# A four-layer image network in one kernel: the second layer's SyncE queue put in written order, two loads moved, a zeroing split

## The chip, the cores and the metric

The kernel runs on one core of a Trainium2 chip. The metric is the device time of one execution in microseconds; lower is better. Single executions are compared by their median.

## What is computed

The input is eight images of 56 x 56 points and 192 channels in fp32. Four layers follow one another, each of the form `x = x + layer(groupnorm(x))`: a gated convolution along rows and columns, an attention over 3 x 3 neighbourhoods, a windowed attention, and a recurrence along rows, columns and diagonals. The change lies in the second layer, whose reference is:

```python
v = x @ Wv
vp = jnp.pad(v, ((0, 0), (1, 1), (1, 1), (0, 0)))
patches = stack of the 9 shifted views of vp at stride 2      # (B, 28*28, 9, 6 heads, 32)
pooled = 2x2 mean of x
a = softmax((pooled @ Wa + ba).reshape(B, 28*28, 6, 9, 9) * scale, axis=-1)
out = einsum('bnhpq,bnqhd->bnphd', a, patches)
y = the 9 parts of out added back at their shifted places     # fold
return y @ Wp + bp
```

## The kernel before, in words

The engines are PE (matrix products), DVE and POOL (element-wise work), ACT (functions and copies) and SP (SyncE), which here only starts DMAs. The second layer, `layer1`, works on 28 units: 4 pairs of images by 7 strips of 8 image rows. Work on a unit is spread over several rounds of one loop over `n` (PE's order within a round is `attend(n)`, the logits of n+2, `values` of n+1, `fold(n)`):

- `load(n)` (L989) brings a unit's input into one of six buffers `x`, with six DMAs. `load(n + 4)` stands first in round n, so it takes the buffer of unit n-2.
- `normalize(n + 3)` applies the group norm on ACT (L1033, three instructions) and pools 2 x 2 points on POOL. `patches(n + 2)` copies nine shifted views into `xc` on DVE, ACT and POOL.
- `attend(n)` multiplies the unit's values `v` by a block-diagonal matrix of attention weights, `bds[n % 2]` (PE, L1155); ACT copies the result out of PSUM into `ys` (L1164).
- `attention(n + 2)` makes the weights: `logits` on PE, DVE and POOL (L1074 to L1085), then `weights` (exponential on ACT L1088, sums on DVE L1089, L1090, product on POOL L1094 into `aq`). SP stores `aq` to a DRAM tile `ad` (L1099), the weights' store.
- `spread(n + 2)` (L1112) reads `ad` back with 14 small DMAs that place the weights on the block diagonals of `bds[n % 2]`. The rest of `bds` is zero and is set to zero once, before the loop.
- `values(n + 1)` (L1126) multiplies the patches by `Wv` in four steps; each needs a bank of PSUM that ACT has to copy out first (L1130).
- `fold(n)` multiplies `ys` by `Wp`, DVE adds it to `x` (L1220), and `finish(n - 1)` stores unit n-1 with six DMAs (L1179) and takes its statistics (L1183). The last strip of a pair finishes its own unit too: twelve stores in that round, none in the next.

Before the loop the first two units are prepared ("the entry"): loads of units 0 to 3, weights of units 0 and 1, and their spreads, which SP and POOL share seven DMAs each. Fetches of norms (L995, L996) and of the next layer's weights (L1279 to L1283) are SP's as well.

The order of the instructions is set in two ways. PE, DVE, ACT and POOL run in the order in which the code is written: `tc.manual_schedule` is entered for them at the top of the layer. SP isn't among them: its DMAs are put in order by a planner, which simulates the kernel with its own costs and issues what it finds ready. An engine executes its queue strictly in order, and an instruction that waits holds up all behind it. SP's first DMA of a spread waits until `ad` has landed in DRAM, and until PE has read the old `bds`; the first DMA of a load waits until the stores of the unit whose buffer it takes have landed. In the third layer's first stage SP is in written order already (L1606).

Of the kernel before, what the change touches and what calls it, by code (L numbers as in the profile page):

```python
# [926 lines left out]
def layer1(cx, xin, xout, w, consts):  # L927
# [9 lines left out]
    tc, nc = cx.tc, cx.nc  # L937
# [5 lines left out]
    NG = 2 * NR  # L943
# [12 lines left out]
    with ExitStack() as es:  # L956
# [13 lines left out]
        E = mybir.EngineType  # L970
# [3 lines left out]
        def parts(x, p, t):  # L974

            cols = slice(t * SW, (t + 1) * SW)
            for i in range(2):
                d = 2 * p + i
                yield x[0:CP, i], d, (slice(None), 0, cols)
                yield x[CP:CA, i], d, (slice(0, CA - CP), 1, cols)  # L980
                yield x[sides[i], 2], d, (slice(CA - CP, None), 1, cols)
# [3 lines left out]
        def load(n, queue=nc.sync):  # L985
            if n < len(units):
                xs[n] = cx.tile(xp, [128, 3, SW], "x")
                for dst, d, at in parts(xs[n], *units[n]):
                    queue.dma_start(dst, xin[d][at])  # L989

        def fetch_norms(p, queue):
            norms[p] = cx.tile(cp, [128, 3, 2], f"norm{p}")
            for i in range(2):
                src = cx.norms[2 * p + i]
                queue.dma_start(norms[p][:, i, :], src[0:CA])  # L995
                queue.dma_start(norms[p][sides[i], 2, :], src[CA:])  # L996
# [24 lines left out]
        bds = [cx.tile(cp, [NP, 2 * NG, NCOL, HEADS, 3], f"bd{i}") for i in range(2)]  # L1021

        def normalize(n):

            p, t = units[n]
            x, xn = xs[n], xns[n % 2]
            if t == 0:
                nc.gpsimd.memset(xn[:, 0, :, 1, :], 0.0)
            else:
                nc.gpsimd.tensor_copy(xn[:, 0, :, 1, :], xns[(n - 1) % 2][:, NR, :, 1, :])  # L1030
            for j in range(3):
                s, o = norms[p][:, j, 0:1], norms[p][:, j, 1:2]
                nc.scalar.activation(  # L1033
                    xn[:, 1:, j, :, 1:], x[:, j].rearrange("p (y i x) -> p y i x", i=2, x=H),
                    AF.Identity, bias=o, scale=s,
                )
            rows = cx.tile(sp, [128, NR, 3, H], "rows")
            nc.gpsimd.tensor_tensor(rows, xn[:, 1:, :, 0, 1:], xn[:, 1:, :, 1, 1:], ALU.add)
            pool4 = cx.tile(wk, [128, 3, NR, N], "pool")
            nc.gpsimd.tensor_tensor(  # L1040
                pool4.rearrange("p j y x -> p y j x"), rows[:, :, :, 0:H:2], rows[:, :, :, 1:H:2], ALU.add
            )
            return pool4.rearrange("p j y x -> p j (y x)")

        def patches(n):

            xn = xns[n % 2]
            xc = cx.tile(wk, [128, 3 * NR, 2, KK, NX], "xc")
            for q in range(KK):
                j, i = divmod(q, 3)  # L1050
                src = xn[:, (i + 1) // 2 : (i + 1) // 2 + NR, :, (i + 1) % 2, j : j + 2 * N - 1 : 2]
                src = src.rearrange("p y j (u x) -> p (y j) u x", u=2)
                dst = xc[:, :, :, q, :]
                if q in (3, 7):
                    nc.gpsimd.tensor_copy(dst, src)
                elif q in (1, 5):
                    nc.scalar.copy(dst, src)
                else:
                    nc.vector.tensor_copy(dst, src)
            return xc  # L1060
# [45 lines left out]
        def spread(n, ad, queues=(nc.sync, nc.sync)):  # L1106

            av = ad.rearrange("i (g x) q f -> x q (i g) f", x=NX)
            bd = bds[n % 2].rearrange("p g c h i -> p g (c h i)")
            for x in range(NX):  # L1110
                at = 2 * x * 3 * HEADS
                queues[x % 2].dma_start(bd[x : x + (KK - 1) * NX + 1 : NX, :, at : at + HK], av[x])  # L1112
# [29 lines left out]
        def attend(n, v):  # L1142


            bd, t = bds[n % 2], units[n][1]
            py = cx.tile(psy, [128, 3, 512], "y")
            for g in range(NG):
                r, half = divmod(g, 2)
                i0 = int(t == 0 and r == 0)
                c0 = int(half == 0)  # L1150
                dims = (NCOL - c0, 3 - i0)
                to = (half * 2 * NX + c0 - 1) * NY + 2 * r + i0
                for k, block in enumerate(blocks):
                    for u, (i, h) in enumerate(block):
                        nc.tensor.matmul(  # L1155
                            sub(py[u * HD : (u + 1) * HD, k, to:], (NY, dims[0]), (1, dims[1])),
                            v[:, i, g, h * HD : (h + 1) * HD],
                            bd[:, i * NG + g, c0:, h, i0:],
                            start=(g == 0), stop=True, skip_group_check=True,
                        )  # L1160
            ys = cx.tile(sp, [128, 3, NY, H], "ys")
            lo = int(t == 0)
            src = py[:, :, 0 : NY * H].rearrange("p j (x y) -> p j y x", y=NY)
            nc.scalar.copy(ys[:, :, lo:, :], src[:, :, lo:, :])  # L1164
            if t:
                nc.gpsimd.tensor_tensor(ys[:, :, 0, :], ys[:, :, 0, :], carry.pop(0), ALU.add)
            if t < NT - 1:
                carry[0] = cx.tile(sp, [128, 3, H], "carry", bufs=2)
                nc.gpsimd.tensor_copy(carry[0], ys[:, :, NY - 1, :])
            return ys  # L1170
# [58 lines left out]
        for i, xn in enumerate(xns):  # L1229
            nc.gpsimd.memset(xn[:, :, :, :, 0], 0.0)  # L1230
        nc.gpsimd.memset(bds[0][:, 0:NG], 0.0)
        pools[0] = normalize(0)
        xcs[0] = patches(0)
        warm = cx.tile(sp, [1, 1], "warm")
# [14 lines left out]
            f()  # L1249
        second = attention(pools.pop(1), ads)  # L1250
        second[0]()
        spread(0, ads.pop(0), (nc.sync, nc.gpsimd))
        vs[1] = cx.tile(wk, [NP, 2, NG, C], "v")
        todo = values(xcs.pop(1), vs[1])
# [3 lines left out]
        pools[2] = normalize(2)  # L1258
        for f in todo:
            f()  # L1260
        nc.vector.memset(bds[1], 0.0)
        spread(1, ads.pop(), (nc.sync, nc.gpsimd))
        gn = cx.gn = GroupNormPairs(cx, cx.keep, w["gmat"])
        gn.place = psb, "b"
# [6 lines left out]
        for n in range(len(units)):  # L1271
            if n == 2:
                for f in cx.late:
                    f(lambda: cx.tile(psb, [128, 512], "b"))
                fetch_norms(NPAIR - 1, nc.sync)
            load(n + 4)
            if n == 20:
                for t, name in zip(cx.held, ("W_vb0", "W_vb1")):
                    nc.sync.dma_start(t, consts[f"l2_{name}"])  # L1279
                nc.sync.dma_start(cx.held[2], consts["l2_b_vb"].partition_broadcast(128))  # L1280
                for i in range(2):
                    nc.sync.dma_start(gn.first[:, i, :], cx.norms[i][0:CA])
                    nc.sync.dma_start(gn.first[sides[i], 2, :], cx.norms[i][CA:])  # L1283
            if n + 3 < len(units):
                pools[n + 3] = normalize(n + 3)
            if n + 2 < len(units):
                xcs[n + 2] = patches(n + 2)
            ys = attend(n, vs.pop(n))
            if n + 1 < len(units):
                todo = []  # L1290
                if n:
                    vs[n + 1] = cx.tile(wk, [NP, 2, NG, C], "v")
                    todo = values(xcs.pop(n + 1), vs[n + 1])
                if n + 2 < len(units):
                    logits, weights = attention(pools.pop(n + 2), ads)
                    logits()
                    todo.insert(2, weights)
                for f in todo:
                    f()
                if ads:  # L1300
                    spread(n + 2, ads.pop())
            if late and late[0][0] <= n:
                late.pop(0)[1]()
            fold(n, ys)
# [1043 lines left out]
def network(tc, d, out):  # L2348
    cx = Ctx(tc)
    B = d["x"].shape[0]  # L2350
    with ExitStack() as es:
        dp = es.enter_context(tc.tile_pool(name="mid", bufs=1, space=DRAM))
        ims = [[d["x"][b] for b in range(B)]]
        for n in range(3):
            ims.append([cx.tile(dp, [CP, 2, HW], f"x{n}_{b}") for b in range(B)])
        ims.append([out[b] for b in range(B)])
        for n, layer in enumerate((layer0, layer1, layer2, layer3)):
            w = {k[3:]: v for k, v in d.items() if k.startswith(f"l{n}_")}
            layer(cx, ims[n], ims[n + 1], w, d)
# [32 lines left out]
```

## Time and profile before

| what | value |
|---|---|
| median of 3 executions | 3863.78 us (3854.99 to 3865.73) |
| the profiled execution's own time | 3867.67 us |
| its span, first to last instruction | 3865.6 us |
| PE busy over the span | 3706.9 us, 96% |
| DVE, ACT, POOL busy | 2421.6, 1806.9, 1535.1 us |
| the second layer | about 1811 to 2445 us |
| starts of `attend`, n = 0 to 6 | 1847.7, 1864.4, 1893.4, 1915.3, 1935.5, 1955.6, 1976.1 us |
| starts of `attend`, n = 23 to 27 | 2344.7, 2365.8, 2387.9, 2409.9, 2429.4 us |
| share of the 16 DMA engines' time, SP's and ACT's queue q1 | 50.0% |

The difference between the profiled time and its span is what lies around the span, 2 us. In the rows of a timeline the first number is the start in us from the span's start, the second the duration; then come engine, line, operation, names as out<-in, and in brackets how long the engine was idle before and what ended it. `SPq` is SP's queue: a row's duration is the issue of the DMAs, not their transfer. Names leave buffer numbers out, so `x<-x` on L989 is a load and on L1179 a store.

### The profile page before, as it was taken

The numbers are of one execution on the slowest core, as the hardware profiler recorded it, in microseconds if no ns is written. First come the engines' busy times: TensorE is split into PE (matmuls) and PEld (weight loads), VectorE is DVE, ScalarE is ACT, GpSimd is POOL, SyncE is SP. The second block draws the span as 40 slices with busy tenths as digits, with TensorE's granted clock in tenths as the row PEclk, the third lists the DMA queues.
The fourth block names the chain that finished last, engine by engine and source line by source line (L and its number), as shares of the span: only waits on it lengthen the run. The fifth ranks groups of instructions, "written<-read, shape, count | busy, mean of one in ns | idle before, by whom it ended". The sixth has DMA issues, their size and how long they took to land. (4 is left out here: it accounts for less than half of the span.)

```text
span 3865.6 us, 116066 instructions
## 1 busy us (share of the span) xinstructions
PE 3706.9 (96%) x51036; PEld 2639.2 (68%) x51036; DVE 2421.6 (63%) x3267; ACT 1806.9 (47%) x2068; POOL 1535.1 (40%) x1336
## 2 busy tenths in 40 slices
PE   7999999999999999998899999899989999999998
PEld 5777878777777868777667666444435555556997
DVE  5657676665757677556444444665657777775665
ACT  4444455444445445344434433344335555554664
POOL 4232242323233242223433333333335545445776
PEclk9999999999999999999999999999999999999999
DMA  8866363434436263343344343656549767664333
GB/s 161 179 137 159 81 168 89 125 98 106 118 85 172 81 160 90 89 101 102 91 124 103 104 97 98 181 174 204 176 146 208 179 162 174 156 151 120 98 111 103
DMA packets 389502, 508.64 MB, mean 132 GB/s; under 512 B 175848, under 2 KB 325672, under 8 KB 387606
## 3 DMA queue, kind: packets, MB, share of 16 engines
q1 hardware_dynamic: 386502, 496.22, 50.0%
q8 instruction: 401, 6.57, 0.7%
q0 software_dynamic: 1424, 4.14, 0.4%
q10 hardware_dynamic: 1072, 0.87, 0.1%
q14 instruction: 103, 0.84, 0.1%
HBM read 345.38 MB, written 155.65 MB: 130 GB/s over the span
## 5 line engine op out<-in xcount | busy, mean ns | idle before, releaser
L438 POOL TENSOR_TENSOR qv<-s,s 128x392 f32<-128x392 f32 (+3 forms) x320 | 564.8, 1796 | 1171.6 <-ACT s L418 796.7
L410 PE MATMUL c<-x,wqv 64*128 64x392 f32 x2592 | 458.4, 497 | 8.4 <-ACT s L418 4.9
L410 PEld LDWEIGHTS c<-x,wqv 64*128 64x128 f32 x2592 | 244.9, 188 | 161.8 <-ACT s L418 6.2
L418 ACT ACTIVATE s<-c,bqv 128x784 f32<-128x784 f32 (+1 forms) x247 | 224.8, 913 | 223.0 <-PE c L410 214.5
L432 DVE TENSOR_TENSOR qv<-s,s 128x784 f32<-128x784 f32 (+1 forms) x160 | 258.9, 1634 | 98.8 <-ACT s L418 98.8
L552 PE MATMUL c<-x,wp 64*128 64x224 f32 x2688 | 282.9, 356 | 14.0 <-ACT s L559 6.8
L471 ACT COPY or<-c 56x1024 f32<-56x1024 f32 x183 | 183.7, 1008 | 222.1 <-DVE ol L471 220.2
L471 DVE COPY ol<-c 56x1024 f32<-56x1024 f32 x184 | 221.7, 1210 | 84.9 <-PE c L465 84.6
L552 PEld LDWEIGHTS c<-x,wp 64*128 64x128 f32 x2688 | 254.8, 189 | 18.7 <-ACT s L559 9.0
L576 DVE TENSOR_TENSOR s<-s,c 128x896 f32<-128x896 f32 x112 | 121.8, 1088 | 219.1 <-ACT s L559 212.8
L1126 PE MATMUL c<-wv,xc 128*126 128x192 f32 (+1 forms) x1792 | 248.9, 336 | 7.0 <-ACT v L1130 4.4
L1126 PEld LDWEIGHTS c<-wv,xc 128*126 128x126 f32 (+1 forms) x1792 | 218.1, 187 | 46.9 <-issue 36.9
L1686 ACT ACTIVATE vb<-sm 128x1024 f32<-128x1024 f32 (+1 forms) x100 | 103.7, 1040 | 258.1 <-issue 220.0
L559 ACT ACTIVATE s<-c,bp 128x448 f32<-128x448 f32 x224 | 129.9, 631 | 190.5 <-PE c L552 189.6
L1835 POOL TENSOR_TENSOR rs<-rs,sin_win 128x896 f32<-128x896 f32 x56 | 136.2, 2450 | 196.5 <-ACT rs L1824 196.5
L510 PEld LDWEIGHTS c<-or,ol 120*64 120x64 f32 (+1 forms) x6720 | 199.6, 133 | 21.4 <-issue 11.1
L510 PE MATMUL c<-or,ol 120*64 120x56 f32 (+1 forms) x6720 | 207.3, 221 | 6.6 <-ACT or L471 5.6
L2257 POOL TENSOR_TENSOR y<-y,s 128x448 f32<-128x448 f32 x164 | 181.4, 1106 | 79.5 <-ACT s L2227 74.7
L1675 PE MATMUL v<-wvb,wa 128*128 128x512 f32 (+1 forms) x400 | 193.2, 615 | 4.9 <-DVE wa L49 4.9
L2214 PE MATMUL h<-ringh,am 128*64 128x57 f32 (+1 forms) x4304 | 184.8, 232 | 7.8 <-DVE ringh L2220 6.1
L1913 ACT ACTIVATE us<-c,bub 128x896 f32<-128x896 f32 x84 | 84.6, 1008 | 222.1 <-PE c L1895 138.9
L1704 POOL TENSOR_TENSOR l<-vb,ta 128x512 f32<-128x512 f32 (+1 forms) x52 | 74.8, 1438 | 275.4 <-ACT vb L1686 275.4
(293 smaller groups left out, 7948.3 us busy)
## 6 DMA issues: line engine op xcount, KB each, us to landing
or<-tt SPq DMA_DIRECT2D x252, 196.0 KB
ol<-tt SPq DMA_DIRECT2D x252, 196.0 KB
vt<-v SPq DMA_DIRECT2D x56, 672.0 KB
v<-vb SPq DMA_DIRECT2D x96, 384.0 KB
x<-x SPq DMA_DIRECT2D x110, 168.0 KB
wqv<-in_l_w_qv SPq DMA_DIRECT2D x40, 384.0 KB
x<-in_x SPq DMA_DIRECT2D x64, 196.0 KB
x<-x SPq DMA_DIRECT2D x110, 112.0 KB
```

Source lines behind the costliest of these rows:

```text
L410: nc.tensor.matmul(ps[:, h, 0:n], wqv[q][rows, k, i, :], xn[rows, k, g * n : (g + 1) * n], start=(k == 0), stop=(k == 2),)
L418: nc.scalar.activation(t, ps[rows, :, 0:n], AF.Silu, bias=bqv[rows, j : j + 1])
L432: nc.vector.tensor_tensor(sub(qv[rows, 7 * g :, 64 + H - 1 :], (HH * 120, 2), (120, 7), (-1, H)), *(t.rearrange("p u (h w) -> p u h w", w= ...
L438: eng.tensor_tensor(sub(qv[rows, w0:, H - 1 - 7 * g - HH * u :], (120, w1 - w0), (-1, 7)), *(t[:, u].rearrange("p (h w) -> p w h", w=H)[:, ...
L471: copy(dst[:, :, :, i0 : i0 + 8], view[rows])
L510: nc.tensor.matmul(ps[u * 64 : u * 64 + m, k, v * H : (v + 1) * H], left[:, d * H : d * H + m], right[:, d * H : (d + 1) * H], start=True, ...
L552: nc.tensor.matmul(ps[:, h, u * n : (u + 1) * n], wps[j][rows, k, u, :], xn[rows, k, g * n : (g + 1) * n], start=(u == 0 and k == 0), stop ...
L1126: nc.tensor.matmul(out(i, u), group(2 if part else i, u)[rows], wv[part][rows], start=(first and u == 0), stop=True, skip_group_check=True,)
L1675: nc.tensor.matmul(out, x[:, at : at + n], wt, start=(k == 0), stop=(k == 1), skip_group_check=True,)
L1835: nc.gpsimd.tensor_tensor(view(b), view(b), tab[1], ALU.mult)
L2214: nc.tensor.matmul((pt if o == 2 else ps)[sides[c], y], am[a][:, o * CB : (o + 1) * CB], old[:, x], start=(m < 2 or (apart and m in (6, 7) ...
L2257: nc.gpsimd.tensor_tensor(v, v, line[0][:, j], ALU.add)
```

## The change

SP is put in written order from the start of the entry's compute to the end of the layer. `load(4)` and `load(5)`, in rounds 0 and 1, move from the start of their rounds to behind that round's spread, `spread(2)` and `spread(3)`. The zeroing of `bds[1]` on DVE, one instruction before, is split in two: the second half of the tile is zeroed earlier, right behind the logits of unit 1. Nothing else is changed; the order of the other engines stays as written.

```diff
         nc.gpsimd.memset(bds[0][:, 0:NG], 0.0)
+        es.enter_context(tc.manual_schedule(engines={E.SP}))
         pools[0] = normalize(0)
...
         second = attention(pools.pop(1), ads)
         second[0]()
+        nc.vector.memset(bds[1][:, NG:], 0.0)
         spread(0, ads.pop(0), (nc.sync, nc.gpsimd))
...
-        nc.vector.memset(bds[1], 0.0)
+        nc.vector.memset(bds[1][:, 0:NG], 0.0)
         spread(1, ads.pop(), (nc.sync, nc.gpsimd))
...
-            load(n + 4)
+            if n > 1:
+                load(n + 4)
             if n == 20:
...
                 if ads:
                     spread(n + 2, ads.pop())
+                if n < 2:
+                    load(n + 4)
             if late and late[0][0] <= n:
```

In written order, a round's DMAs on SP are `load(n + 4)`, the weights' store of n+2, `spread(n + 2)`, and the stores of unit n-1.

## The prediction

> **What bounds the kernel now.** I read the windows by stage first, then PE's waits, then SP's queue row by row, because the change touches the second layer (about 1811 to 2445 us) and nearly all of it concerns SP. Durations are from the profiled execution.
>
> ```profile
> 1845.00:1915.00 70.00, 58.25 (x801) 41.66 (x800) 33.59 (x49) 26.30 (x35) 32.76 (x43) 0.93 0.34 87
> 1915.00:2344.00 429.00, 416.68 (x5658) 296.70 (x5656) 192.38 (x334) 173.77 (x227) 156.85 (x194) 0.99 0.43 108
> ```
> Columns: length, then busy time of PE, weight loads, DVE, ACT, POOL. In the long middle PE is busy 416.68 of 429.00 us: PE sets the pace there. `attend` begins at 1915.33 (n=3) and 2344.74 (n=23), which is 21.47 us per unit; a plain unit takes 20.1 (1915.33 to 1935.45), the ones that carry group-norm steps about 22. Only the entry has idle PE worth naming: 11.75 of 70 us.
>
> ```profile
> PE y L1155 <- DMA bd<-ad: 4.4, 2, 2.8
> PE c L1126 <- ACT v L1130: 4.4, 3, 2.3
> ```
> These are the largest waits of PE from 1915 to 2410: only 4.4 us for spreads. So there is little for a better order to win. SP's queue in the same stage, in order of time (start, length):
>
> ```profile
> 1931.34 3.14 SPq L1179 DMA_DIRECT2D x<-x  x6
> 1934.58 0.52 SPq L1099 DMA_DIRECT2D ad<-aq  x1
> 1935.20 0.43 SPq L1179 DMA_DIRECT2D x<-x  x1
> 1936.40 3.67 SPq L989 DMA_DIRECT2D x<-x  x6
> 1940.17 11.22 SPq L1112 DMA_DIRECT2D bd<-ad  x14
> 1951.44 2.73 SPq L1179 DMA_DIRECT2D x<-x  x5
> 1954.53 0.32 SPq L1099 DMA_DIRECT2D ad<-aq  x1
> ```
> L1179 is a unit's store, L1099 the weights' store, L989 the input's load, L1112 the spread. SP issues for 18 to 19 of the 20 us of a round: it is almost full. The planner's order is ad, one store, six loads, spread, five stores. It matters because two waits hide behind other issues: the spread reads what ad wrote and must wait until it landed (the loads lie in between), and load(n+4) takes the buffer of x(n-2), so must wait until that unit's six stores landed (ad lies in between; 0.6 us of the wait is left, at 1936.22).
>
> **The change, part by part.** *Written order.* In a round SP will now do load(n+4), ad(n+2), spread(n+2), stores of n-1, and again load. Both landings stand open. What a landing costs when nothing lies between:
>
> ```profile
> 1872.02 0.34 SPq L1099 DMA_DIRECT2D ad<-aq  x1
> 1875.12 11.14 SPq L1112 DMA_DIRECT2D bd<-ad  x14
> ```
> ```profile
> 2017.33 3.30 SPq L989 DMA_DIRECT2D x<-x  x6
> 2020.74 0.53 SPq L1099 DMA_DIRECT2D ad<-aq  x1
> ...
> 2024.62 10.88 SPq L1112 DMA_DIRECT2D bd<-ad  x14
> ```
> From ad's issue to the spread: 3.10 us on an empty queue, 3.88 right behind six loads; the same distance at 2170.80, 2303.41 and 2328.62 is 4.58, 4.24, 3.58. I take 4.1, the mean of the four behind loads, as that is where ad will stand; ends 3.1 and 4.6. From the last store's end to the load of its buffer: 1934.48 to 1936.40, 1.9 (1.5 to 2.3). A round then is: loads 3.1 (the rows that follow a wait have 2.96 to 3.12; back to back 3.7 to 4.2) + 0.1 + 4.1 + spread 11.0 (10.84 to 11.69) + 0.05 + stores 3.1 + 1.9 = 23.25 us. At a pair's end the stores of two units go together, which saves one landing in seven rounds (-0.27), and four norm stores of 0.5 are added (+0.3): 23.3. PE's pace is 21.47, so SP becomes the bound. While SP has slack in hand nothing shows; spread(5) was issued by 1951.39 and is in at about 1953 (POOL's spreads land 2.2 us after their issue), `attend(5)` began at 1955.62: a slack of some 2.5 us. The units from `attend(6)` to `attend(25)` are 19 rounds: 19 x 23.3 = 442.7, before 2387.87 - 1976.14 = 411.7; with the seven fetches of n=20 (W_vb, b_vb, norms; 7 x 0.5, today issued in SP's pauses) +3.6. Sum **+35 us**; with 22.3 a round +16, with 24.2 +52. Queued behind each open wait are the other three kinds of SP's DMAs; who waits is PE (`attend` for spreads) and ACT (`normalize` for loads).
>
> The Trainium skill, "DMA: Bandwidth & Descriptors", section "Rules for kernel authors", speaks against the change: issue a DMA early and wait on it late. The same page ("Anatomy of one DMA") puts a DMA's fixed cost at about 2.0 us; an estimate with it in place of 4.1 would shorten the round to about 21.1 and leave next to nothing of the +35. The rows say 3.1 to 4.6 for this 435 KB store, and I go by them.
>
> *The entry's loads.* load(4) and load(5) are issued today between 1838.50 and 1854.57, well before their use. Now load(4) stands behind spread(2), load(5) behind spread(3). First the gain, in order of the written queue:
>
> ```profile
> 1852.00 0.52 SPq L1099 DMA_DIRECT2D ad<-aq  x1
> ...
> 1857.02 4.18 POOL L1112 DMA_DIRECT2D bd<-ad  x7 [7.00 <-DMA ad<-aq]
> ...
> 1864.42 5.87 PE L1155 MATMUL y<-bd,v 126*32 126x84 f32 x192 [3.69 <-DMA bd<-ad]
> ...
> 1867.62 2.06 ACT L1033 ACTIVATE xn<-x,norm 128x448 f32<-128x448 f32 x3
> ...
> 1870.40 1.40 ACT L1164 COPY ys<-y 128x1512 f32<-128x1512 f32 x1
> ...
> 1875.29 0.80 ACT L1130 COPY v<-c 126x768 f32<-126x768 f32 x1 [3.48 <-PE c L1126]
> ```
> ad(1) waits behind loads until 1852.00, though POOL finished aq at 1847.57. It now goes at 1847.6, lands about 1851.6, spread(1) is in by 1859, and `attend(1)` starts when PE is free at 1860.8: 3.7 us won. POOL, freed 5 us earlier, lets ad(2) go at 1866.8 instead of 1872.02. Then the loss: landing 3.4 to 1870.2, spread(2) 11.1 to 1881.3, load(4) from 1881.3; its last part is in 5.6 us after the first issue (load(6): issue 1916.24, last `normalize` step released at 1921.90), so at 1886.9. On ACT `normalize(4)` (1867.62 today) stands ahead of ys(1) and the four copies that empty PSUM for `values(2)`. ACT stands still until 1887.8; patches 0.9, ys 1.4, the first copy 0.8: PE, which can do two `values` steps without it, goes on at 1890.9. Two more steps and a wait for a bank 4.7, `fold` 4.4: 1900.0 instead of 1887.45, +12.6. For unit 2 the same: ad(3) 1899.1, spread(3) to 1913.8, load(5) in by 1919.5, normalize to 1920.3, PE resumes at 1923.4 where it could at 1918, and the group bank adds some; `attend(3)` at about 1932.5 instead of 1915.33: **+17 us** (10 if the parts land at 3 us, 22 if each transfer is as slow as 2170.80). SP stays late and reaches its bound at `attend(6)`, another +1.5.
>
> *Half of the zeroing.* DVE waits 4.48 us before L1089 at 1843.36; a half costs 3.54 (L1240), starting 0.8 to 1.7 after its predecessor. Cost 0; without that cover ad(1) is up to 0.8 us later. The other half ends by 1851, before spread(1). The Trainium skill, "SBUF — State Buffer", section "Who interferes with whom", names DVE copies in a two-port mode as what holds up POOL's own DMA issues. An estimate with the moved half as such an instruction would delay spread(0)'s POOL half by up to 3.5 us. No row here shows DVE zeroing against POOL's issues; the rows show POOL's additions at their usual 1.39 us under L1240.
>
> *Moved without cost.* Eight norm fetches (8 x 0.5) leave their place around ad(0) for SP's pause before ad(2). At the exit ident and the first two tables, today at 2432.98, go behind the last twelve stores (2448.72); DVE's L1645 would wait from 2449.90 to about 2453, hidden since DVE's next bias addition waits for PE until 2455.97: 0 to +2, I take 1.
>
> Sum: 17 + 1.5 + 35 + 1 = +54.5 on 3867.67 us. The median is 3.9 below that execution, so against it 3863.78 + 54.5 = about 3918.
>
> **The rivals.** *Only the entry pays.* If ad lands in about 2 us and the stores' landing is mostly covered, the round is 21.2, under 21.47, and only the +17 remains: 3881. For it: landings under light DMA load could be shorter. Against: none of the ten such distances in this stage is under 3.1.
>
> *Faster: SP keeps pace and the planner's disorder goes.* At pair ends the planner issues eleven stores in a row (7.71 us at 2158.67), after which a spread comes late and PE waits 2.83 and 1.55; with the ACT waits of 4.4, and 3.7 at the entry with the slow clock behind it (`attend(1)` 5.87 instead of 4.56), up to 13.8 us: 3850. It decides if the round stays under 20.1 (3.15 of the 6.0 us of open landings would have to vanish) and load(4) and load(5) come in time. Against it: load(4) cannot be issued before ad(2) landed, and that needs work of POOL after 1861.
>
> *No change.* The planner's order is close to the written one already; if the waits moved cost what the entry wins, or the order were not imposed on SP, the time stays at 3864.
>
> **How the numbers follow.** What a measurement of this kernel can tell from no change is about 0.3%, 11.6 us. Chances: SP bound 0.74, entry alone 0.14, faster 0.06, no change 0.06. The first lies wholly above 11.6; of the second 0.01 falls within. Slower 0.87, same 0.07, faster 0.06. The likeliest's own range: entry 10 and round 22.3 give 3863.8 + 10 + 16 = 3890; entry 22, round 24.2, exit 2 and 4 for what the planner rearranges later give 3863.8 + 80 = 3944. The low end goes down to 3877 to take in most of the entry-alone case; the high end stays at 3944.
>
> **What would show it.** Right: the rows of SP's queue read L989 x6, L1099, pause of about 3.5, L1112 x14, L1179 x6, pause of 1.9, with starts of L1112 some 23 us apart; PE waits for bd<-ad in most units, 1 to 3 us each; ACT L1033 at the entry waits over 12 us for x<-x. Wrong: `attend` starts still 20.1 apart in plain units, or pauses before L1112 under 2 us (then only the entry counts), or `normalize(4)` with its x in time before 1875 (then the +17 falls).

## The result and the profile after

The changed kernel takes 3934.77 us in the median of four executions (3929.54 to 3936.58); the kernel before, four executions in the same session, 3859.54 us (3854.99 to 3865.73). The ratio is 1.0185 (95% interval 1.0171 to 1.02): slower, by about 75 us. The profiled execution of the changed kernel took 3929.54 us, its span is 3927.4 us, PE is busy for 3717.1 us of it (95%).

Where the time arose can be read from the starts of `attend` in the two traces:

| stretch | before, us | after, us | difference | predicted |
|---|---|---|---|---|
| start of the kernel to `attend(0)` | 1847.7 | 1839.1 | -8.6 | 0 |
| `attend(0)` to `attend(3)`, the entry | 67.6 | 85.7 | +18.1 | +17 |
| `attend(3)` to `attend(6)` | 60.8 | 62.1 | +1.3 | +1.5 |
| `attend(6)` to `attend(25)`, 19 rounds | 411.7 | 463.4 | +51.7 | +35 |
| `attend(25)` to the end | 1477.7 | 1477.1 | -0.6 | +1 |

The first row isn't the change's: the 8.6 us arise between 195 and 255 us, in the first layer, where the two kernels have the same instructions. So the second layer cost about 70 us, although the two profiled executions differ by only 61.9.

**The windows by stage**, the two of before again (length; busy time of PE, weight loads, DVE, ACT, POOL; granted clock, DMA share, GB/s):

```profile
1845.00:1915.00 70.00, 44.46 (x552) 31.01 (x550) 20.50 (x38) 16.53 (x22) 21.61 (x29) 0.83 0.25 62
1915.00:2344.00 429.00, 387.62 (x5098) 274.94 (x5100) 174.13 (x304) 157.68 (x207) 142.91 (x180) 0.97 0.36 94
```

PE was busy for 416.68 of the 429 us and now for 387.62; in the entry for 44.46 where it had 58.25. DMA traffic fell from 108 to 94 GB/s, and the DMA engines' mean busy share from 0.43 to 0.36: the engines stand idle longer than before, so the loss doesn't look like one of bandwidth.

**SP's queue**, a round without a pair's end (start, time of issue, number of DMAs):

```profile
2060.05 3.06 SPq L989 DMA_DIRECT2D x<-x  x6
2063.22 0.53 SPq L1099 DMA_DIRECT2D ad<-aq  x1
2067.40 10.88 SPq L1112 DMA_DIRECT2D bd<-ad  x14
2078.39 3.12 SPq L1179 DMA_DIRECT2D x<-x  x6
2083.40 3.40 SPq L989 DMA_DIRECT2D x<-x  x6
```

Read it by its gaps. From ad's start at 2063.22 to the spread at 2067.40 the queue issues only for the first 0.53 us; from the stores' end at 2081.51 to the load at 2083.40 it issues nothing. Everything else follows without a pause, and the round takes 2083.40 - 2060.05 = 23.35 us, where PE needs 20 to 22. SP's own waits over the layer, before (first fence, 1845 to 2450) and after (1845 to 2530; columns: waiter and what it waited for, us in total, times, longest):

```profile
SPq L1112 <- DMA ad<-aq: 16.3, 12, 2.7
...
SPq L989 <- DMA x<-x: 2.3, 5, 0.6
```
```profile
SPq L1112 <- DMA ad<-aq: 81.5, 26, 4.5
SPq L989 <- DMA x<-x: 31.3, 28, 4.1
```

Both landings that the planner had hidden, 18.6 us together, stand open now: 112.8 us. The chain of waits that ended last, from `attend(6)` to `attend(25)`, by line:

```profile
by line: SPq L1112 21.9%; PE c L1126 13.5%; DMA x<-x 11.5%; SPq L989 9.2%; SPq L1179 7.8%; DMA ad<-aq 6.3%; issue 5.5%; PE y L1155 4.1%; PE c L1201 3.3%; PE c L1197 1.7%; PE c L1074 1.6%; PE b L1356 1.4%; PE b L1203 1.4%; ACT xc L1057 1.3%;
```

SP's issues (21.9 + 9.2 + 7.8) and the landings of DMAs (11.5 + 6.3) make 57% of it. PE's waits after, 1845 to 2530:

```profile
PE c L1126 <- ACT v L1130: 50.9, 18, 19.0
PE y L1155 <- DMA bd<-ad: 12.6, 6, 5.3
PE y L1155 <- issue: 5.9, 8, 1.7
```

PE loses most not at `attend` for a spread but in `values`, for ACT's copies of PSUM: 50.9 us, of which 31.9 from 1915 on. ACT is no busier than before (214.05 us from `attend(0)` to `attend(25)`, before 215.59); it stands at `normalize(n + 3)` for a late load, and ys and the copies are queued behind that. ACT's waits for loads, before (1845 to 2450) and after (1845 to 2530):

```profile
ACT xn L1033 <- DMA x<-x: 180.5, 40, 12.4
```
```profile
ACT xn L1033 <- DMA x<-x: 289.2, 49, 22.0
```

Before, ACT had time for such waits: PE lost only 4.4 us for its copies. After, the chain shows in the loop too. PE is in round 6, and SP issues `load(9)`, which belongs to round 5, only now:

```profile
1991.81 3.84 SPq L989 DMA_DIRECT2D x<-x  x6
1995.02 0.76 ACT L1033 ACTIVATE xn<-x,norm 128x448 f32<-128x448 f32 x1 [12.24 <-DMA x<-x]
...
1999.42 1.40 ACT L1164 COPY ys<-y 128x1512 f32<-128x1512 f32 x1
2000.73 1.49 ACT L1130 COPY v<-c 126x768 f32<-126x768 f32 x2
2001.58 6.25 PE L1126 MATMUL c<-wv,xc 64*126 64x192 f32 x32 [2.37 <-ACT v L1130]
```

The entry shows the whole of it (in brackets how long the engine stood idle before, and what ended it):

```profile
1844.65 4.18 POOL L1112 DMA_DIRECT2D bd<-ad  x7 [3.02 <-DMA ad<-aq]
...
1851.39 4.55 PE L1155 MATMUL y<-bd,v 126*32 126x84 f32 x192
...
1859.66 0.33 SPq L1099 DMA_DIRECT2D ad<-aq  x1
...
1862.87 11.57 SPq L1112 DMA_DIRECT2D bd<-ad  x14
...
1874.49 3.12 SPq L989 DMA_DIRECT2D x<-x  x6
1877.41 0.76 ACT L1033 ACTIVATE xn<-x,norm 128x448 f32<-128x448 f32 x1 [22.02 <-DMA x<-x]
...
1882.66 1.50 ACT L1130 COPY v<-c 126x768 f32<-126x768 f32 x2
...
1883.52 6.08 PE L1126 MATMUL c<-wv,xc 64*126 64x192 f32 x32 [19.04 <-ACT v L1130]
```

Spread(1) waits 3.02 us for ad where it waited 7.00, and `attend(1)` (L1155) starts 12.3 us after `attend(0)` instead of 16.7, without a wait. Then the price: load(4) is issued at 1874.49, behind the 14 DMAs of spread(2); ACT has stood for 22.02 us at 1877.41; PE, whose PSUM ACT should have emptied, for 19.04 at 1883.52.

### The profile page after: what moved, and what is told of

The parts are those of the page before. It is cut to its first block, busy times and chain, and to the rows that moved or that the text cites. A ratio compares the mean times of both kernels' runs of the same rounds, so it can differ in the third digit from the quotient of the medians.

```text
span 3927.4 us, 116094 instructions
## 1 busy us (share of the span) xinstructions
PE 3717.1 (95%) x51036; PEld 2644.5 (67%) x51036; DVE 2416.8 (62%) x3268; ACT 1804.5 (46%) x2068; POOL 1532.9 (39%) x1336
## 4 chain that ended last, share of the span: by engine, by line
PE 37%; SPq 6%; DMA 3%; issue 2%; DVE 1%; ACT 1%; POOL 1%; POOLq 0%; DVEq 0%; ACTq 0%
PE v L1680 6%; PE h L2219 4%; PE c L1943 3%; PE c L1882 3%; PE c L1891 3%; SPq L1112 3%; PE kv L1740 3%; PE c L1126 2%; PE c L1900 2%; PE c L1910 2%; PE b L1931 2%; DMA x<-x 1%; SPq L989 1%; PE y L1155 1%; SPq L1179 1%
## 5 line engine op out<-in xcount | busy, mean ns | idle before, releaser
L1126 PE MATMUL c<-wv,xc 128*126 128x192 f32 (+1 forms) x1792 | 260.6, 345 | 52.5 <-ACT v L1130 50.9
L1033 ACT ACTIVATE xn<-x,norm 128x448 f32<-128x448 f32 x84 | 62.1, 760 | 305.1 <-DMA x<-x 303.4
```

The source lines that it names most:

```text
L1126: nc.tensor.matmul(out(i, u), group(2 if part else i, u)[rows], wv[part][rows], start=(first and u == 0), stop=True, skip_group_check=True,)
```

## The experiments

All edits are against the changed kernel, unless another is named. The first four ran on one chip (before there: 3869.23 us), the last four on another (before: 3867.03 us); ratios are to before on the same chip. Theory: in written order a round on SP lasts longer than PE's, because both landings lie open (A), and the two loads behind the spreads cost once more at the entry (B). Rivals: the entry alone pays; the moved zeroing gets in the way of POOL; loads that are late only matter because SP never catches up.

**1. The two loads back at the start of their rounds** (`e1_loads_first`), SP still in written order.

```diff
-            if n > 1:
-                load(n + 4)
+            load(n + 4)
...
-                if n < 2:
-                    load(n + 4)
```

> The changed kernel with load(4) and load(5) put back to the start of rounds 0 and 1; SP stays in written order. Theory (an entry loss of 17 to 18 us from late loads, and a round of SP that is too long): ACT's normalize(4) finds its x in time, the stretch from attend(0) to attend(3) falls from 85.8 us to about 68 to 70 (67.6 in the kernel before), while the rounds of SP stay at 24.4; since SP's lag catches up with PE within a few rounds, only 10 to 18 us of the 71 come back: about 3917 to 3925. Rival (the two moved loads are the whole of it): about 3860 to 3870. Rival (the written order alone, the moved loads cost nothing): about 3935.

Measured: 3927.47 us, ratio 1.0145 (1.013 to 1.016), so 0.4% (15.5 us) less than the changed kernel's 1.0185. The time lies just above the 3917 to 3925 expected. `attend(0)` to `attend(3)` falls from 85.7 to 61.8 us, further than the 68 to 70 expected, but the following stretches give 13 of these 24 us back: `attend(3)` to `attend(6)` 67.7, `attend(6)` to `attend(25)` 470.7. By the stretches 11 us are left. The loads' place is the smaller part; "the entry alone pays" falls.

**2. SP back under the planner** (`e2_planner`), loads and zeroing as changed.

```diff
-        es.enter_context(tc.manual_schedule(engines={E.SP}))
```

> The changed kernel without the one line that puts SP in written order: the planner orders SP, the two loads stand behind their spreads in the text, the zeroing is split. Theory: the planner issues loads when it finds them ready, wherever they stand in the text, so nothing of the loss is left: within 10 us of the kernel before, 3850 to 3870. Rival (the place of the loads in the text is what costs): the stretch from attend(0) to attend(3) stays near 85 us and the time is 3875 or more.

Measured: 3869.03 us, ratio 1.0001 (0.999 to 1.0012); `attend(0)` to `attend(3)` 66.0 us, `attend(6)` to `attend(25)` 414.4. With this one line gone the whole loss is gone. The moved loads and the split zeroing alone cost nothing: the planner issues the twelve DMAs of load(4) and load(5) between 1835.08 and 1850.72 us, ahead of spread(1), as it did before (1838.50 to 1854.57).

**3. Written order, with load(n + 4) between the weights' store and the spread** (`e3_load_behind_ad`).

```diff
-            if n > 1:
-                load(n + 4)
...
+                load(n + 4)
                 if ads:
                     spread(n + 2, ads.pop())
-                if n < 2:
-                    load(n + 4)
```

> Written order, but in every round load(n + 4) stands between the weights' store and the spread; so the landing of the weights' store lies behind the load, and the landing of the stores behind the weights' store. Nothing else changes. Theory (two open landings in each round): a round of SP comes to 18.5 to 20 us, PE sets the pace again (21.5 per unit, attend(6) to attend(25) in about 410 instead of 463.5), at the entry load(4) is 11 us earlier, so about 3855 to 3872. Rival (any strict order costs, since SP cannot pick what is ready): over 3900. Rival (the loads' lateness, not SP's sum, is the cost): here a load is issued some 18 us later within its round than in the changed kernel's text, so rounds of 24 or more stay and the time is 3930 or more.

Measured: 3864.02 us, ratio 0.9985 (0.9976 to 0.9995): the loss turns into a gain of 5 us that its interval holds off from 1. `attend(6)` to `attend(25)` takes 409.2 us (before 411.7). SP's queue in this kernel, one round:

```profile
1970.46 0.32 SPq L1099 DMA_DIRECT2D ad<-aq  x1
1971.09 3.28 SPq L989 DMA_DIRECT2D x<-x  x6
1974.47 11.50 SPq L1112 DMA_DIRECT2D bd<-ad  x14
1986.08 3.12 SPq L1179 DMA_DIRECT2D x<-x  x6
1991.10 0.32 SPq L1099 DMA_DIRECT2D ad<-aq  x1
```

The same DMAs in the same number: the six loads now lie where the queue stood open for ad, and the spread follows them after 0.10 us. The stores land while the queue waits for the new aq (1989.20 to 1991.10). So it is not written order as such that costs, but this written order: A is shown in its two landings together.

**4. A seventh buffer for x** (`e4_seven`): load(n + 4) takes the buffer of x(n - 3), whose stores landed long ago. The place comes from one buffer less of `aq` and of `carry`.

```diff
-        xp = pool("l1x", 6)
+        xp = pool("l1x", 7)
...
-                aq = cx.tile(wk, [TW, 2, KK, HK], "aq")
+                aq = cx.tile(wk, [TW, 2, KK, HK], "aq", bufs=1)
...
-                carry[0] = cx.tile(sp, [128, 3, H], "carry", bufs=2)
+                carry[0] = cx.tile(sp, [128, 3, H], "carry", bufs=1)
```

> The changed kernel with seven buffers for x instead of six (room is made by one buffer instead of two for the weights and for the carried row): load(n + 4) takes the buffer of unit n-3, whose stores landed a round ago. The order is unchanged. Theory: the wait from stores to load, 2.45 us a round, goes, the landing of the weights' store, 3.7, stays: rounds of 22 us, attend(6) to attend(25) about 420 to 430 instead of 463.5, about 3893 to 3905. Rival (only the weights' store is waited for): stays at 3930. Rival (the late load through ACT is all): about 3875, the entry's loss alone.

Measured: 3921.67 us, ratio 1.0131 (1.0115 to 1.0147), more than the 3893 to 3905 expected. The pause between stores and loads is down to 0.10 us, the one behind ad stays; `attend(6)` to `attend(25)` takes 442.2 us, 21 us less than in the changed kernel, but more than the 420 to 430 expected. The plain rounds are as expected: spreads start at 2070.72, 2092.64 and 2114.82, 21.9 and 22.2 us apart. Most of the rest sits in the two rounds with norm stores, 29.7 and 29.3 us from spread to spread:

```profile
2147.39 0.42 SPq L1391 DMA_DIRECT2D norm<-nn  x1
2147.86 0.51 SPq L1392 DMA_DIRECT2D norm<-nn  x1
2148.72 0.34 SPq L1391 DMA_DIRECT2D norm<-nn  x1
2149.11 0.48 SPq L1392 DMA_DIRECT2D norm<-nn  x1
2149.71 8.06 SPq L1179 DMA_DIRECT2D x<-x  x6
2157.86 4.71 SPq L989 DMA_DIRECT2D x<-x  x6
```

Six stores behind four norm stores take 8.06 us instead of 3.1, and 8.25 at 2313.56. That makes some 15 us in two rounds. Within the 8.06 us single issues took 2.33 and 3.56 us; why wasn't tried.

**5. The changed kernel once more** (`after_again`), so that the next three stand beside it on one chip.

> The changed kernel itself once more, so that the following three stand beside it on one chip. Theory (written order costs 50 us in the rounds of SP and 18 us at the entry): ratio to the kernel before 1.017 to 1.020, as in its first runs.

Measured: 3943.39 us, ratio 1.02 (1.0187 to 1.0213), at the upper end of what was expected; entry 85.2 us, `attend(6)` to `attend(25)` 465.8.

**6. The zeroing in one piece again** (`e7_zero_whole`).

```diff
-        nc.vector.memset(bds[1][:, NG:], 0.0)
...
-        nc.vector.memset(bds[1][:, 0:NG], 0.0)
+        nc.vector.memset(bds[1], 0.0)
```

> The changed kernel with the zeroing of bds[1] in one instruction again, at its old place. Theory: the split costs and brings nothing, since the moved half (3.54 us of DVE) lies in DVE's idle time and ends before spread(1): within 3 us of the changed kernel, ratio to before 1.016 to 1.020. Rival (a DVE zeroing beside POOL's half of spread(0) holds up POOL's DMA issues): the moved half costs up to 3.5 us at attend(0), which this would give back, and the seven POOL issues of spread(0) would get shorter than the 4.28 us that they took beside the zeroing.

Measured: 3942.64 us, ratio 1.02 (1.0187 to 1.0213), the same as the run before it. POOL's half of spread(0) and DVE's zeroing, first with the zeroing split (`after_again`), then whole:

```profile
1844.45 4.28 POOL L1112 DMA_DIRECT2D bd<-ad  x7
```
```profile
1843.31 3.54 DVE L1253 MEMSET bd<- 126x4176 f32 x1 [0.82 <-issue]
1849.83 3.54 DVE L1263 MEMSET bd<- 126x4176 f32 x1 [0.82 <-ACT v L1130]
```
```profile
1838.94 4.28 POOL L1112 DMA_DIRECT2D bd<-ad  x7
```

The first zeroing (1843.31 to 1846.85) lies beside POOL's seven issues; they take 4.28 us with it and 4.28 without. The estimate that the prediction drew from the Trainium skill ("SBUF — State Buffer", "Who interferes with whom"), up to 3.5 us if this instruction were of the kind that holds up POOL's issues, doesn't hold for it: nothing is held up.

At spread(1) the split is worth something. With the tile zeroed in one piece, POOL's half of spread(1) waits for the zeroing:

```profile
1845.18 7.02 DVE L1262 MEMSET bd<- 126x8352 f32 x1 [1.69 <-ACT v L1130]
1852.50 4.18 POOL L1112 DMA_DIRECT2D bd<-ad  x7 [4.38 <-DVE bd L1262]
```

`attend(1)` then starts 13.9 us after `attend(0)`, in `after_again` 11.9. The medians of the two kernels don't show these 2.0 us.

**7. The entry's price alone** (`e8_entry_late`): the loop's loads behind ad as in experiment 3, load(4) and load(5) behind the spreads as changed.

```diff
-            if n > 1:
-                load(n + 4)
...
+                if n > 1:
+                    load(n + 4)
                 if ads:
                     spread(n + 2, ads.pop())
                 if n < 2:
                     load(n + 4)
```

> Written order with the loop's loads from n=2 on behind the weights' store (both landings hidden, as in the third experiment) and load(4), load(5) behind spread(2), spread(3) as in the changed kernel: the entry's price alone. Theory: attend(0) to attend(3) 83 to 87 us as in the changed kernel (before 67.6), attend(6) to attend(25) 408 to 413 (before 411.7): 10 to 16 us over the kernel before, ratio 1.0025 to 1.0045. Rival (the entry's delay only matters because SP's full queue never gives it back; an SP with slack catches up and the ACT waits shrink): attend(6) is back to within 5 us of before, ratio 0.999 to 1.001.

Measured: 3881.98 us, ratio 1.0037 (1.0024 to 1.0051). `attend(0)` to `attend(3)` 87.1 us, `attend(6)` to `attend(25)` 410.5. B is shown: the late loads cost some 20 us at the entry by the stretches (14 by the ratio, whose interval allows 9 to 20), and with a queue that has slack nearly nothing of it comes back later and nothing is added.

**8. The same loop with load(4) and load(5) right behind spread(1), before the loop** (`e5_entry_early`), the version that the experiments point to.

```diff
         spread(1, ads.pop(), (nc.sync, nc.gpsimd))
+        load(4)
+        load(5)
...
-            if n > 1:
-                load(n + 4)
...
+                if n > 1:
+                    load(n + 4)
                 if ads:
                     spread(n + 2, ads.pop())
-                if n < 2:
-                    load(n + 4)
```

> The same loop, with load(4) and load(5) issued right behind spread(1), before the loop: the version that the experiments point to. Theory: attend(0) to attend(3) falls from the 69.1 us of the third experiment to 61 to 65 (the spreads of the entry come early, which the changed kernel showed at attend(1), and the loads are in before normalize(4) wants them), the rounds stay at 21.5 us each: ratio to before 0.996 to 0.998, the fastest of all. Rival (the loads delay ad(2) and spread(2), which then set attend(2)): attend(0) to attend(3) 66 to 70, ratio 0.998 to 1.000.

Measured: 3859.91 us, ratio 0.9982 (0.9973 to 0.9991), some 7 us faster than before and 83 faster than the changed kernel. The ratio lies just above the 0.996 to 0.998 expected. The entry takes 61.8 us, as expected, 6 less than before. The 19 rounds take 412.7 us, 3.5 more than in experiment 3, so the totals of the two (0.9982 and 0.9985) can't be told apart. PE's waits from 1915 to 2450:

```profile
PE c L1126 <- ACT v L1130: 7.1, 5, 3.5
PE y L1155 <- issue: 6.1, 9, 1.5
```

No wait for a spread is left, and those for ACT are down from 31.9 us (the changed kernel from 1915 on) to 7.1.

**The sum from the runs.** Experiment 8 and the changed kernel differ by 83 us on one chip, 3943.39 - 3859.91. The entry is 0.0055 of it (1.0037 - 0.9982), 21 us. Experiment 4 has the late entry and ad's landing open, but not the stores': against experiment 7 it has 0.0094 more, 36 us, and the changed kernel 0.0054 to 0.0069 more than experiment 4 (by which of its two ratios one takes), 21 to 27 us. So: entry 21, ad's landing 36, stores' landing 21 to 27. The intervals leave each of these uncertain by some 6 to 8 us, and the runs stand on two chips. These are prices in this order of removal; a kernel with only the stores' landing open wasn't run, and experiment 4 also has one buffer less of two small tiles.

## Why the prediction was right, and where its sizes were off

The forecast was slower, 3918 us in 3877 to 3944; it is 3934.77, inside the range, and by the mechanism named first, SP as the bound. In change it was 54.5 us forecast against 70.5 measured by stretches (75 by medians); nearly all of the miss is the rounds' term.

**Written order.** The mechanism is shown by experiments 2 and 3; the size was 51.7 us and not 35. The term that was mis-sized is the length of a round. I put it together from the best or middle rows of a queue that had slack. In the changed kernel, mean over the rounds from 1985 to 2450: six loads 3.5 us (I took 3.1), ad to spread 3.7 (4.1), spread 10.96 (11.0), six stores 3.8 (3.1), stores to load 2.45 outside the pair ends (1.9). Three terms were 0.4 to 0.7 too low, one 0.4 too high, and 23.3 became 24.4 us a unit (463.4 / 19), or 24.2 without the 3.6 us that I had added for the fetches of n = 20. The excess of stores and pauses isn't spread evenly: about half of it stands in the two rounds with norm stores (one pause of 4.67 us, one group of stores of 7.62), which I had put in with 0.3 us of issue only. The top of the range, 24.2 us a round, was reached.

**Landing.** From ad's start to the spread it was 3.3 to 4.3 us in these rounds. The price of about 2.0 us that the Trainium skill gives for a DMA's fixed cost ("DMA: Bandwidth & Descriptors", "Anatomy of one DMA") would have made the round 21.1 us, inside PE's pace; the rows of before were the better guide. That section fits the price to DMAs that POOL issues, and adds a part that grows with the bytes, which I left out: as an estimate by its formula, 2.0 + bytes / 436e3, the 435 KB of ad take 3.0 us, near the 3.10 on an empty queue, and the round would be about 22.2 us. What lies queued ahead of ad isn't in it. That page's rule on issuing early and waiting late ("Rules for kernel authors") held: 36 us of experiment 4's time against that of experiment 7 are the price of breaking it for ad alone.

**Entry.** +17 predicted, +18.1 in the profile, and by steps: `attend(1)` 4.4 us nearer to `attend(0)` than before (3.7 of waiting predicted); ACT free of `normalize(4)` and its copies done such that PE resumes 44.4 us after `attend(0)` (43.2 predicted); `attend(3)` at 85.7 (84.8). In the last of these two misses partly cancel: counted from `attend(0)`, PE ended `fold(1)` 15.0 us later than before (12.6 predicted), and unit 2 added only 3.1 (4.6 predicted). The forecast sign "ACT L1033 waits over 12 us for x<-x" came at 22.02.

**Zeroing** at nothing: experiment 6 for the total; the 2.0 us that the split wins at `attend(1)` weren't foreseen. **Exit** at +1: -0.6.

**Wrong: the place of PE's waits.** The prediction wanted them at `attend`, 1 to 3 us for bd<-ad in most units. There are six such waits in the layer. It treated load and spread as two customers of a late queue and priced the round, which was enough for the time; but the load comes first in the round, its lateness reaches ACT, and PE finds ACT's copies missing before it gets to the next spread. At the entry I had followed this very chain; in the loop I didn't carry it on.

**The rivals.** "Only the entry pays" needed a round under 21.47 us; that kernel exists as experiment 7, and costs 14 us by its ratio where 17 were priced. "Faster: SP keeps pace" is close to experiments 3 and 8: where the round stays short and the loads come in time, written order does win, 5 to 7 us of the 13.8 set as the most. The condition I named for it (3.15 of 6.0 us of open landings must vanish) was what one line's place decides. "No change" is experiment 2, by the planner.

## What to carry to other kernels

When a queue is taken from a planner and written by hand, list for every waiting DMA what lies between it and what it waits for; a wait costs the landing less that distance. Place a batch that is ready anyway (here six loads) between a store and the DMAs that read it back: with that the same 27 DMAs per round went from 24.4 us to PE's own 21.5. When a queue becomes the bound, add up its round from rows of a loaded queue, at their mean and not at their best, and look for the rare small DMAs in it.

## What the runs showed that I had not expected

**PE's own work got longer when it waited.** From `attend(0)` to `attend(25)`, before, changed, and experiment 8:

```profile
1847.70:2387.90 540.20, 517.19 (x7026) 368.26 (x7027) 247.68 (x422) 215.59 (x282) 204.06 (x255) 0.98 0.41 105
```
```profile
1839.10:2450.40 611.30, 532.22 (x7024) 377.30 (x7024) 240.96 (x422) 214.05 (x282) 203.54 (x256) 0.95 0.35 92
```
```profile
1846.80:2383.30 536.50, 517.92 (x7026) 367.60 (x7030) 237.79 (x422) 214.61 (x282) 205.48 (x254) 0.99 0.43 106
```

The same 7024 to 7026 matrix products took 532.22 us instead of 517.19, at a granted clock of 0.95 instead of 0.98; with the waits gone (experiment 8) it is 517.92 at 0.99. So of the 71 us between these two starts 56 are idle time of PE and 15 are slower work. Where SP sets the round, slower work only fills time that PE would have waited; how much of the 15 us counts wasn't separated.

**A stall that comes and goes.** The 8.6 us by which the changed kernel's profile is early at `attend(0)` belong to the first layer, and on the second chip its `attend(0)` is at 1851.0, with the same code. A difference of two profiled executions is read from the starts of a stage, not from the totals.
